# A spectral convolution's mode mix with x stationary and weights streaming, in a four-layer kernel on one core

## The chip, the core and the metric

The kernel runs on one core of a Trainium2 chip. The core has a matrix engine (TensorE, PE; its loads of the stationary operand are listed apart as PEld), a vector engine (DVE), a scalar engine (ACT), GpSimd (POOL), a queue engine (SP) that issues DMA transfers, and 16 DMA engines that all queues share. SP, ACT and POOL each have a queue of transfers of their own. The metric is the device time of one execution in microseconds (us). All data are float32; a float32 matmul of the program appears in the trace as two load and matmul pairs.

## The reference, cut to what matters

The input x is 8 x 32 x 256 x 256. Four layers follow one another, each adding to x a function of its group-normalised value. The change lies in the first and touches the start of the second:

```python
def _L0_conv_ref(x, w1r, w1i, w2r, w2i, bias):      # x: group-normalised
    w1 = w1r + 1j * w1i                              # 32 x 32 x 32 x 32: in, out, ky, kx
    w2 = w2r + 1j * w2i
    x_ft = jnp.fft.rfft2(x)
    out_lo = jnp.einsum('bixy,ioxy->boxy', x_ft[:, :, :M1H, :M2H], w1)
    out_hi = jnp.einsum('bixy,ioxy->boxy', x_ft[:, :, -M1H:, :M2H], w2)
    ...
    out = jnp.fft.irfft2(out_ft, s=(h, w))
    return out + bias
...
x = x + _L0_conv_ref(_gn(x), ...)                    # layer 0
x = x + _L1_conv_ref(_gn(x), L1_conv_kernel, 1, 2)   # layer 1: one 5 x 5 kernel for every channel
```

So for each of 64 x 32 modes there is a small complex product: 8 batches by 32 input channels, times 32 x 32 weights of that mode. Layers 2 (a recurrence over columns) and 3 (running maxima in four directions and a 1 x 1 convolution) are not touched.

## The kernel before, in words

**Forward (forward_and_mix, L75).** Work goes in 64 units: 8 batches of 8 units of 4 channels. A unit's x is 1 MB; `load(u)` (L113) brings it on SP into a ring of AHEAD = 7 buffers. `over_columns(u)` (L118) makes 16 matmuls (L131), one sum of squares on ACT (L140) and one on DVE (L141), and a transpose of the result on DVE (L144). `over_rows` (L148, matmuls at L158) transforms the second axis for the batch before, in four slices, so a batch's units 0 to 3 carry a slice each; its stationary operand is the table `fh` (1 MB, loaded at L107). `turn` (L166) transposes, `statistics` (L179) finds mean and scale, and `normalise` (L198) scales by DVE (L201), writes the modes with a sign to `xf[:, 0]` by ACT (L202), and the swap of real and imaginary parts to `xf[:, 1]` by four DMAs on POOL (L206). Lines L210 to L245 write the order of all this out by hand: every engine executes its instructions in that order.

**Constants (load_consts, L39).** SP issues eleven loads of constants first (L44), then `fh`, and then x.

**Mix (L247 to L290).** kx goes in 8 groups q of KC = 4. The weights of a q are 2 MB: q=0 has a pool of its own and is loaded in the last forward batch (L216); the next five buffers take space that the forward has to release first, and are loaded in a row when it ends (L253); two more follow. For each ky, pair of kx and half s (low or high ky), one matmul (L269) has the weights as its stationary operand (64 rows, 2 kx x 32 outputs) and x's modes as the moving one (32 columns: real and imaginary, batch, 2 kx). ACT (L286) and DVE (L284) copy the results out of PSUM into `sm`, two buffers per half, and SP and ACT store them to the DRAM tensor `smd`, laid out `[B, 2, KM, C, 2, KM]`: pieces of 256 B.

**Inverse and convolution (inverse_and_conv, L297).** `load_spectrum(b)` (L346) reads the modes of a batch back: 64 rows at once (L351), and the same with real and imaginary parts exchanged, in pieces of 128 B, in two more DMAs (L353). `turn` negates a half (L358), `means` (L364) and `spectrum` (L367 to L381) work on the zero mode. The tile's name in the profile is spec. `over_rows` (L403) then uses slices of spec as the stationary operand of the matmuls tp (L410), 512 instructions in all, and `over_columns` (L419) finishes the inverse transform (up, L427) and adds x, read a second time as xb (L388, issued on POOL, six DMAs of 786 KB for a unit). `conv` (L478) is layer 1. The order is again written out by hand, L613 to L689: spectra 0 and 1, the first unit's xb, then the first tp.

The DMA of the constant `bias` (L322) stands ahead of the spectrum loads in SP's queue, and its tile reuses space of the mix.

Of the kernel before, what the change touches and what calls it, by code (L numbers as in the profile page):

```python
# [38 lines left out]
def load_consts(tc, pool, d):  # L39
    nc = tc.nc  # L40
    k = Consts()
    for name in ("sign", "sel", "msel", "fw", "gw", "eh", "ident", "ident32", "pair", "valid", "conv"):
        t = pool.tile(list(d[name].shape), F32, name=f"c_{name}")
        nc.sync.dma_start(out=t, in_=d[name])  # L44
        setattr(k, name, t)
# [29 lines left out]
def forward_and_mix(tc, k, d, smd, xmean):  # L75
# [12 lines left out]
    with ExitStack() as ctx:  # L88
        one = ctx.enter_context(tc.tile_pool(name="m1", bufs=1))
        wp = ctx.enter_context(tc.tile_pool(name="mw", bufs=1))  # L90


        xf = one.tile([P, 2, B, KM, KM], F32, name="xf")
        wts = {}

        def load_weights(q, wp):
            wts[q] = wp.tile([P, KM, KC, C], F32, name=f"wt_{q}", tag="wt")
            nc.sync.dma_start(out=wts[q].rearrange("p y j o -> p (y j o)"), in_=d["wm"][q])

        with ExitStack() as inner:  # L100
            fwd = inner.enter_context(tc.tile_pool(name="a1c", bufs=1))
            xp = inner.enter_context(tc.tile_pool(name="a1x", bufs=AHEAD))
# [4 lines left out]
            nc.sync.dma_start(out=fh, in_=d["fh"])  # L107
# [90 lines left out]
            def normalise(b):  # L198
                xb, rs = turned.pop(b)
                xb = xb.rearrange("p y x -> p (y x)")  # L200
                nc.vector.tensor_scalar_mul(xb, xb, rs)  # L201
                nc.scalar.activation(xf[:, 0, b].rearrange("p y x -> p (y x)"), xb, AF.Copy, scale=k.sign)  # L202
                for s in range(2):
                    for ri in range(2):
                        r, r2 = 64 * s + 32 * ri, 64 * s + 32 * (1 - ri)
                        nc.gpsimd.dma_start(  # L206
                            out=xf[r : r + 32, 1, b].rearrange("p y x -> p (y x)"), in_=xb[r2 : r2 + 32]
                        )

            with tc.manual_schedule(engines=None):  # L210
                for u in range(AHEAD - 1):
                    load(u)
                for u, (b, n) in enumerate(units):
                    if u + AHEAD - 1 < len(units):
                        load(u + AHEAD - 1)
                    if b == B - 1 and n == 2:  # L216
                        load_weights(0, wp)
# [10 lines left out]
                    if b == B - 1 and n == NK - 2:  # L228
                        for i in range(SLICES):
                            over_rows(b, i, 0, NK // 2)  # L230
                for i in range(SLICES):
# [15 lines left out]
        wp2 = ctx.enter_context(tc.tile_pool(name="mw2", bufs=5))  # L247
        sp = ctx.enter_context(tc.tile_pool(name="ms", bufs=2))
        ps = ctx.enter_context(tc.tile_pool(name="mp", bufs=4, space=PSUM))
        NQ = KM // KC  # L250
        KY = KM // 2
        with tc.manual_schedule(engines=None):
            for q in range(1, 6):  # L253
                load_weights(q, wp2)
            for q in range(NQ):
                if 2 <= q < 4:
                    load_weights(q + 4, wp2)
                wt = wts.pop(q)
                mps = [
                    [ps.tile([P, 2 * B, 2, KY], F32, name=f"mp_{q}_{s}_{h}", tag=f"mp{s}") for h in range(2)]  # L260
                    for s in range(2)
                ]


                for ky in range(KM):
                    for j in range(0, KC, 2):
                        for s in range(2):
                            r = slice(64 * s, 64 * s + 64)
                            nc.tensor.matmul(  # L269
                                mps[s][ky // KY][32 * j : 32 * j + 64, :, :, ky % KY],  # L270
                                lhsT=wt[r, ky, j : j + 2, :].rearrange("p j o -> p (j o)"),
                                rhs=xf[r, :, :, ky, KC * q + j : KC * q + j + 2].rearrange("p r b x -> p (r b) x"),
                                start=True,
                                stop=True,
# [1041 lines left out]
```

## Time and profile before

| what | us |
|---|---|
| time of three runs, median (lowest to highest) | 3023.08 (3022.15 to 3023.44) |
| the profiled execution: its time | 3029.68 |
| the profiled execution: span from first to last instruction | 3027.8 |
| first x has landed, first matmul | 14.6 |
| last matmul of the forward's row transform ends | 208.1 |
| mix: first matmul; from here without a break | 216.37; 217.35 |
| mix: last matmul ends, first xb issued | 293.1, 293.66 |
| first load of a spectrum issued | 310.38 |
| first tp matmul | 321.44 |

Over the whole span PE is busy 92%, DVE 85%, ACT 62%, POOL 29%; the granted PE clock is 0.96 of full speed in the mean. Times in views are us from the start of the span, unless a number is marked ns. In the windows view a row is one stretch, with the busy time and the number of instructions of each engine; PEclk is the clock granted to PE. A line of the waits view says which engine's instruction at which line sat waiting for what, in total, how often, and the longest. Two passes make a matmul, so 1024 matmuls of the mix are 2048 instructions. Matmuls overlap in the array, so an instruction's own duration is longer than the time from one to the next. Beside the views, the trace has a record of every DMA packet: its start, queue, size and the time that it took.

### The profile page before, as it was taken

The page shows a single profiled execution, that of the slowest core. Times are in us where ns is not written, and L with a number is a line of the kernel's source. Part 1 is how long each engine was busy: PE and PEld are TensorE (multiplying, and loading weights), DVE is VectorE, ACT ScalarE, POOL GpSimd, SP SyncE. Part 2 cuts the span into 40 slices and gives each one's busy share as a digit, 9 for nine tenths or more (in the row PEclk, how much of TensorE's full clock was granted, in tenths as well). Part 3 has the DMA queues.
Part 4 walks back from the last instruction along what each step waited for, and adds up shares of the span by engine and source line. Part 5 has one row for each costly group of instructions (what it writes and reads, how often), then busy time and mean ns, then how long its engine had stood idle before and what let it go on. Part 6 is the DMA issues. An engine that isn't in the chain of part 4 may idle for free.

```text
span 3027.8 us, 111688 instructions
## 1 busy us (share of the span) xinstructions
PE 2784.2 (92%) x47736; PEld 1643.4 (54%) x47736; DVE 2578.6 (85%) x5161; ACT 1864.6 (62%) x4471; POOL 886.4 (29%) x1270
## 2 busy tenths in 40 slices
PE   7986799999999899999999999999999588888887
PEld 4656344444444566666666666666666333333333
DVE  5753578788788699999999999999999999999997
ACT  3432477767777688888888888888888232222222
POOL 0110122112221555555555555555555300000000
PEclk9995899999999899999999999999999799999998
DMA  9977678777776576566766566556764598888885
GB/s 386 392 274 241 181 214 241 227 216 228 220 224 173 140 169 154 141 142 156 169 145 142 141 164 162 143 141 148 169 153 114 185 376 326 323 325 326 331 333 225
DMA packets 470049, 655.69 MB, mean 217 GB/s; under 512 B 328016, under 2 KB 332000, under 8 KB 443312
## 3 DMA queue, kind: packets, MB, share of 16 engines
q1 hardware_dynamic: 410112, 484.48, 55.0%
q0 software_dynamic: 16224, 82.28, 8.2%
q10 hardware_dynamic: 43216, 81.79, 7.6%
q8 instruction: 374, 6.13, 0.8%
q14 instruction: 123, 1.01, 0.1%
HBM read 371.63 MB, written 272.63 MB: 213 GB/s over the span
## 4 chain that ended last, share of the span: by engine, by line
PE 66%; DVE 19%; issue 4%; DMA 2%; ACT 1%; SPq 0%; POOL 0%; DVEq 0%; ACTq 0%; POOLq 0%
PE r L784 14%; PE z L784 13%; PE vp L498 12%; PE ni L784 7%; PE nh L784 7%; DVE rv L1070 4%; PE up L427 4%; DVE dq L1085 2%; DVE uq L1087 2%; DVE m L1096 2%; DVE m L1093 2%; DVE m L1090 2%; PE tp L410 2%; PE mp L269 2%; PE o L1102 1%
## 5 line engine op out<-in xcount | busy, mean ns | idle before, releaser
L792 PE MATMUL z<-hs,weights 64*64 64x256 f32 x4080 | 539.4, 382 | 0.0
L792 PE MATMUL r<-hs,weights 64*64 64x256 f32 x4080 | 525.5, 375 | 0.0
L876 POOL TENSOR_TENSOR xw<-xw,hs 128x256 f32<-128x256 f32 x496 | 340.0, 686 | 632.8 <-DVE hs L875 629.7
L792 PE MATMUL ni<-hs,weights 64*64 64x256 f32 x4080 | 524.9, 375 | 0.0
L1128 ACT ACTIVATE ot<-o,bres 128x512 f32<-128x512 f32 x256 | 155.1, 688 | 493.4 <-PE o L1102 478.8
L498 PE MATMUL vp<-x,c_conv 64*64 64x384 f32 (+5 forms) x4608 | 424.2, 490 | 7.9 <-DVE x L531 7.9
L531 DVE SCALAR_TENSOR_TENSOR x<-vp,r,x 128x128 f32<-128x128 f32 (+2 forms) x640 | 350.4, 562 | 89.6 <-PE vp L498 77.5
L868 POOL TENSOR_TENSOR a<-zm,xn 128x256 f32<-128x256 f32 x510 | 373.0, 731 | 4.3 <-ACT zm L861 4.3
L866 ACT ACTIVATE n<-n,bih 128x256 f32<-128x256 f32 x510 | 259.2, 508 | 182.8 <-DVE n L865 182.8
L784 PE MATMUL r<-hs,weights 64*64 64x256 f32 x2040 | 319.1, 389 | 1.1
L498 PEld LDWEIGHTS vp<-x,c_conv 64*64 64x64 f32 x4608 | 222.2, 132 | 179.5 <-issue 101.5
L784 PE MATMUL z<-xn,weights 64*64 64x256 f32 x2040 | 305.3, 376 | 9.8 <-ACT xn L764 9.8
L1102 PE MATMUL o<-m,wsc 32*32 32x512 f32 x3072 | 226.2, 713 | 95.8 <-DVE m L1096 92.9
L784 PE MATMUL r<-xn,weights 64*64 64x256 f32 x2040 | 305.8, 376 | 0.0
L784 PE MATMUL nh<-xn,weights 64*64 64x256 f32 x2040 | 305.7, 376 | 0.0
L784 PE MATMUL z<-hs,weights 64*64 64x256 f32 x2040 | 305.4, 376 | 0.0
L784 PE MATMUL ni<-hs,weights 64*64 64x256 f32 x2040 | 305.2, 375 | 0.0
L764 ACT ACTIVATE xn<-xw,shift,turned 128x256 f32<-128x256 f32 x492 | 288.2, 586 | 0.0
L792 PEld LDWEIGHTS ni<-hs,weights 64*64 64x64 f32 x4080 | 284.4, 133 | 0.3
L860 DVE SCALAR_TENSOR_TENSOR n<-nh,bhh,rs 128x256 f32<-128x256 f32 x510 | 246.3, 483 | 43.1 <-ACT rs L859 28.2
L792 PEld LDWEIGHTS r<-hs,weights 64*64 64x64 f32 x4080 | 281.2, 131 | 0.2
L859 ACT ACTIVATE rs<-r,brz 128x256 f32<-128x256 f32 x510 | 241.7, 474 | 58.9 <-PE r L792 36.7
(171 smaller groups left out, 6243.4 us busy)
## 6 DMA issues: line engine op xcount, KB each, us to landing
xb<-in_xl_dram POOLq DMA_DIRECT2D x96, 768.0 KB, 7.2
xa<-in_xt_dram SPq DMA_DIRECT2D x64, 1024.0 KB
fwd<-fm SPq DMA_DIRECT2D x256, 256.0 KB
out_dram<-ot ACTq DMA_DIRECT2D x64, 1024.0 KB
xw<-x2d SPq DMA_DIRECT2D x248, 256.0 KB
fw<-fwd SPq DMA_DIRECT2D x31, 2048.0 KB
x3d<-xw SPq DMA_DIRECT2D x240, 256.0 KB
x<-x3d SPq DMA_DIRECT2D x30, 2048.0 KB
```

The source lines that it names most:

```text
L498: ins = nc.tensor.matmul(vps[bank][to, :, dst], lhsT=k.conv[r, P : P + 64] if kind == 2 else k.conv[r, o], rhs=pair_of(u, ch, g, lo, hi, s ...
L531: nc.vector.scalar_tensor_tensor(x, src[o], r1[rows, g : g + 1], x, ALU.mult, ALU.add, accum_out=s1[rows, 0, n, ch, g : g + 1])
L764: nc.scalar.activation(norms[bi][:, b, w], raws[bi][:, b, w], AF.Identity, bias=shift[:, b : b + 1], scale=sc[:, 1, b : b + 1])
L784: ins = nc.tensor.matmul(out[r], lhsT=weights[r, kind, gate, :], rhs=src[r], start=start, stop=stop)
L792: ins = nc.tensor.matmul(out[pairs[1 - i]], lhsT=weights[r, kind, gate, :], rhs=prev[r, :, q0 : q0 + Q], start=False, stop=stop,)
L859: rs = nc.scalar.activation(r, p["r"], AF.Sigmoid, bias=brz[:, 0:1])
L860: nc.vector.scalar_tensor_tensor(m, p["nh"], bhh[:, 2:3], r, ALU.add, ALU.mult)
L866: nc.scalar.activation(m, m, AF.Tanh, bias=bih[:, 2:3])
L868: product = nc.gpsimd.tensor_tensor(a, zm, cur, ALU.mult)
L876: nc.gpsimd.tensor_tensor(raw, raw, new, ALU.add)
L1102: nc.tensor.matmul(banks[bi][b2][i][32 * j : 32 * j + 32].rearrange("p (w q) -> p w q", q=Q), lhsT=wsc[q, b2, t, :], rhs=src[j][q, b2], st ...
L1128: nc.scalar.activation(ot[:, i], banks[bi][b2][i], AF.Identity, bias=bres[:, b2, i : i + 1])
```

## The change

- **Mix.** The stationary operand is now x's modes: for one ky and one q, 64 rows by 64 columns (real and imaginary, 8 batches, 4 kx), contiguous in a new layout of `xf`. The moving operand is the weights of the four kx, 128 columns. The result holds every x of the four kx against every weight of the four; only the blocks with equal kx are stored. A q is worked in two blocks c of 1 MB of weights, each in two groups of 4 ky per half.
- **Weights in x's ring.** Weights come in 16 halves of 1 MB through the same seven buffers and the same queue as x: seven halves behind the last x, each further one when a block of the mix has released a buffer.
- **Results.** A group's results are copied with one instruction for each s (128 x 512) into a stage tile, two buffers per s; `smd` is laid out `[2, KM, 2, 2, B, KM // 2, C]`, so that a stored row is 2 KB; eight DMAs of 64 KB for a q, four on SP and four on POOL. A spectrum is read in rows of 2 KB; the first on three queues. tp's stationary operand is then a slice with a step of 32 elements.
- **Order.** `fw` and six units of x are issued ahead of `fh`; three small constants follow between x's loads, the others and `bias` behind the weights at the forward's end. The first unit's xb is issued on SP within the mix (q = 5), from a pool of its own. The halves of `xf` with real and imaginary parts exchanged are made by copies on ACT (in the last batch on DVE, POOL and ACT) and not by DMAs. The first spectrum's half is negated on ACT.
- **Pools.** Those of the convolution wait for single tiles (`reuse_waits="tile"`).

```diff
-        nc.sync.dma_start(out=t, in_=d[name])
-        setattr(k, name, t)
+        setattr(k, name, pool.tile(list(d[name].shape), F32, name=f"c_{name}"))
+    k.bias = pool.tile([P, C], F32, name="bias0")
+    def load(*names):
+        for name in names:
+            nc.sync.dma_start(out=getattr(k, name), in_=d[name])
...
-        xf = one.tile([P, 2, B, KM, KM], F32, name="xf")
+        xf = one.tile([P, KM, KM // KC, 2, B, KC], F32, name="xf")
...
+        def load_weights(i):
+            if i < 2 * NQ:
+                q, h = divmod(i, 2)
+                wts[i] = xp.tile([P, 2, KY // 2, KC, C], F32, name=f"wt_{q}_{h}", tag="xa")
+                size = KY * KC * C
+                nc.sync.dma_start(
+                    out=wts[i].rearrange("p h y j o -> p (h y j o)"), in_=d["wm"][q, :, h * size : (h + 1) * size]
+                )
...
-                        nc.gpsimd.dma_start(
-                            out=xf[r : r + 32, 1, b].rearrange("p y x -> p (y x)"), in_=xb[r2 : r2 + 32]
-                        )
+                        out, src = xf[r : r + 32, :, :, 1, b], xb[r2 : r2 + 32]
+                        if b < B - 1 or s and ri:
+                            nc.scalar.copy(out, src)
+                        else:
+                            (nc.gpsimd if s else nc.vector).tensor_copy(out, src)
...
+                k.load("fw")
                 for u in range(AHEAD - 1):
                     load(u)
+                nc.sync.dma_start(out=fh, in_=d["fh"])
+                small = ["sign", "sel", "msel"]
                 for u, (b, n) in enumerate(units):
                     if u + AHEAD - 1 < len(units):
                         load(u + AHEAD - 1)
-                    if b == B - 1 and n == 2:
-                        load_weights(0, wp)
+                        if u > 1 and small:
+                            k.load(small.pop(0))
+                    else:
+                        load_weights(u + AHEAD - 1 - len(units))
...
+                load_weights(AHEAD - 1)
+                k.load("gw", "eh", "ident", "ident32", "pair", "valid", "conv")
+                nc.sync.dma_start(out=k.bias, in_=d["b0"].partition_broadcast(P))
...
             for q in range(NQ):
...
+                stage = [sp.tile([P, KC, KY, C], F32, name=f"sm_{q}_{s}", tag=f"sm{s}") for s in range(2)]
+                for c in range(2):
+                    wt = wts.pop(2 * q + c)
+                    for i in range(0, KY // 2, 4):
+                        mps = [ps.tile([P, 4, KC, C], F32, name=f"mp_{q}_{c}_{i}_{s}", tag=f"mp{s}") for s in range(2)]
+                        for y in range(4):
+                            for h in range(2):
+                                for s in range(2):
+                                    r, to = slice(64 * s, 64 * s + 64), slice(64 * h, 64 * h + 64)
+                                    ky = KY * h + KY // 2 * c + i + y
+                                    nc.tensor.matmul(
+                                        mps[s][to, y].rearrange("p j o -> p (j o)"),
+                                        lhsT=xf[r, ky, q].rearrange("p r b x -> p (r b x)"),
+                                        rhs=wt[r, h, i + y].rearrange("p j o -> p (j o)"),
+                                        start=True,
+                                        stop=True,
+                                    )
...
+                            dst, src = stage[s][:, :, ky : ky + 4], mps[s].rearrange("p y j o -> p j y o")
                             if s:
                                 nc.vector.tensor_copy(dst, src)
                             else:
                                 nc.scalar.copy(dst, src)
+                    load_weights(AHEAD + 2 * q + c)
+                if AHEAD + 2 * q in (2 * NQ, 2 * NQ + 1):
+                    for i in range(3):
+                        xb(0, 0, 0, i, nc.sync)
+                for s in range(2):
+                    for m in range(KC):
+                        (nc.sync, nc.gpsimd)[m % 2].dma_start(
+                            out=smd[s, KC * q + m].rearrange("h r b y o -> (h r b) (y o)"),
+                            in_=stage[s][m::KC, m].rearrange("p y o -> p (y o)"),
+                        )
...
+def conv_x(nc, d, pool):
...
+    def load(u, b, h, i, queue):
+        lo, hi = 3 * i, 3 * i + 3
+        for ch in range(2):
+            t = pool.tile([P, hi - lo, CH, Q], F32, name=f"xb_{u}_{ch}_{i}", tag=f"xb{ch}{i}")
+            queue.dma_start(
+                out=t.rearrange("p t c q -> p (t c q)"), in_=d["xl"][b, 2 * h + ch, :, lo * CH * Q : hi * CH * Q]
+            )
...
         def load_spectrum(b):
...
+            t = spp.tile([P, 2, 2, KM // 2, C], F32, name=f"spec_{b}", tag="spec")
+            queues = (nc.sync, nc.scalar, nc.gpsimd) if b == 0 else 3 * (nc.scalar if b > 1 else nc.sync,)
+            modes = smd[:, :, :, :, b].rearrange("s x h r y o -> (s x) h r (y o)")
+            flat = t.rearrange("p h r y o -> p h r (y o)")
+            queues[0].dma_start(out=flat[0:64].rearrange("p h r n -> p (h r) n"), in_=modes.rearrange("p h r n -> p (h r) n"))
             for ro in range(2):
-                queue.dma_start(out=t[64:128, :, ro], in_=modes[:, :, 1 - ro])
+                queues[ro + 1].dma_start(out=flat[64:128, :, ro], in_=modes[:, :, 1 - ro])
...
-                        lhsT=specs[b][:, 2 * CH * h + CH * ch + c + j].rearrange("p r y -> p (r y)"),
+                        lhsT=specs[b].rearrange("p h r y c -> p (h r y) c")[:, :, 2 * CH * h + CH * ch + c + j],
...
-            for i in range(3):
-                load(0, i)
-            turn(0, nc.vector)
+            half = specs[0][64:128, :, 1]
+            nc.scalar.activation(half, half, AF.Copy, scale=-1.0)
```

The host's layouts of the weights and of the table `gw` follow the new order; the amount of data is the same.

## The prediction

> **What bounds the kernel now.** I cut the span into stages with the windows view (us; busy time and count of PE, PEld, DVE, ACT, POOL; granted clock; DMA share; GB/s):
>
> ```profile
> 0.00:14.63 14.63, 0.00 (x0) 0.00 (x0) 0.91 (x7) 1.28 (x1) 2.02 (x7) 1.00 0.81 280
> 14.63:216.37 201.74, 186.97 (x3234) 119.46 (x3235) 136.72 (x266) 82.12 (x136) 26.89 (x40) 0.99 0.92 358
> 216.37:293.10 76.73, 57.53 (x2048) 55.71 (x2048) 25.22 (x60) 21.88 (x61) 0.00 (x0) 0.52 0.72 243
> 293.10:321.44 28.34, 0.61 (x2) 0.50 (x2) 3.35 (x11) 1.39 (x4) 3.37 (x8) 0.50 0.91 242
> 321.44:950.00 628.56, 618.60 (x7154) 291.99 (x7154) 507.77 (x1585) 445.37 (x1362) 120.10 (x153) 1.00 0.75 219
> ```
>
> These are: waiting for the first x; the forward transform; the mix; a gap in which smd is stored and read back; the convolution. Only these are touched. The convolution is 98% PE: nothing but a slower PE, or a later start, matters there. So the start of its first matmul (tp, 321.44) is the number to predict; everything later moves with it.
>
> The forward by batches of 8 units, then the waits (engine, line, who ended them: total, times, longest):
>
> ```profile
> 14.70:36.80 22.10, 18.44 (x289) 10.62 (x289) 15.78 (x26) 10.28 (x18) 0.00 (x0) 1.00 1.01 426
> 60.30:83.80 23.50, 23.03 (x396) 14.53 (x392) 17.02 (x34) 10.23 (x17) 3.56 (x5) 1.00 1.01 389
> ```
> ```profile
> PE y L364 <- DMA spec<-smd: 25.5, 1, 25.5
> PE yp L131 <- DMA xa<-in_xt_dram: 18.4, 7, 14.7
> ACT sm L286 <- DMA smd<-sm: 9.5, 1, 9.5
> SPq L322 <- DMA smd<-sm: 14.4, 1, 14.4
> ```
>
> The first batch goes at the pace of x (1 MB in 2.44 us by the arrivals, 426 GB/s); from the second on PE is the bound (23.03 of 23.50). PE waits 14.7 us for the first x and 25.5 for the spectrum. The third line is a store of q=0, still under way when its buffer is wanted at q=2: it was issued at 225.2, while five weight loads of 2 MB from 217.5 on stood in the DMA engines.
>
> **Part by part**, against the profiled execution (3029.68 us, span 3027.8; the shown median is 3023.08, 6.6 less; I carry the difference over).
>
> 1. *First x ahead.* Now SP issues 11 constants and fh before x, from 0.75 to 6.40, and x lands at 14.63. After: fw, then x. SP issues x at about 1.2; in the packet records data follow some 1.4 us after an issue; 1 MB takes 2.44, the 384 KB of recurrence weights beside it 0.9, and before, a landing showed 1.0 after its last packet: 7.0. That is 7.6 earlier, but fh now stands between x number 6 and 7, in the batch that goes at x's pace: 2.44 back. **-5.2.** (Bounds: 0, if the second batch were to wait for fh, to -7.6.)
>
> 2. *xf by copies.* Four POOL DMAs a batch become four ACT copies of 32x1024. The nearest row is the sign copy (L202, 1.15 us): 4.6 a batch. ACT is busy 10.24 of 23.50 and sits in front of the ring, waiting for x; the ring of 7 gives back what one late release costs, since x needs 8 x 2.44 = 19.5 of 23.5. So 0. Runs of 4 elements are new: at twice the price, 9.2, it still fits in the 13.3 that are free; from 3.3 us a copy on it would cost. In the last batch two copies go to DVE, one to POOL, one to ACT. POOL's row (L358, 1024 elements) is 2.78: from the end of DVE's scaling (212.68) dense mixing can start at about 215.8 instead of 217.35. **-1.6.**
>
> 3. *The mix itself.* 2048 PE instructions of 64x32 become 1024 of 64x128 (8 x 2 x 2 x 4 x 2 x 2 matmuls, two passes each). Now the first 254 took 6.31 us, 24.8 ns each, later ones 28.4 (128 in 3.64): a floor of an instruction and not of its columns. The recurrence issues 1824 instructions of 64x256 in its windows row 1500 to 1600, 54.8 ns each at clock 1.00; half the columns: 27.4. So 1024 x 27.4 = 28.1 us, and 56 at clock 0.50. Which clock?
>
> ```profile
> 212.70:222.90 10.20, 6.67 (x220) 6.33 (x221) 2.15 (x6) 2.60 (x5) 1.99 (x4) 0.51 0.65 202
> 222.90:226.30 3.40, 1.45 (x81) 1.26 (x73) 1.68 (x4) 1.45 (x4) 0.00 (x0) 0.97 1.01 424
> 226.30:293.00 66.70, 50.11 (x1766) 48.65 (x1765) 21.86 (x52) 18.91 (x52) 0.00 (x0) 0.50 0.70 235
> ```
>
> The clock came once, after 5.5 us of the densest stretch, and stayed at 0.50 through 66.7 us in which PE was busy 75%. With four times the columns per instruction the array has work all the time at 0.50, so I take cold for 5.5 us and warm after: 16 blocks, two or three of 3.4 us, then 1.85. [...]
>
> 4. *Its DMA is the new bound.* The ring holds 7 of the 16 half weights when mixing starts: their loads follow the releases of units 57 to 63. Left after that: 9 x 1.05 MB weights, 4.72 MB of conv's first xb (six of 786 KB, now queued on SP at q=5), 4.19 MB of stores: 18.4 MB at 0.42 MB/us, 43.7 us. The first release comes at 3.4, data 1.5 later: all moved at about 48.5, while PE alone could be done at 33. Stores of 2 KB rows: such packets (x2d) took 84 ns in the convolution, 24 GB/s an engine, near the 26.5 of 8 KB packets. In the recurrence they took 152, which would add 8 us. I take 84, the same direction and kind.
>
> 5. *The tail.* SP's half of the stores of q=5 is queued behind xb in the same ring. Stage tiles are double, so the evacuation of q=7 waits for them, as L286 did for 9.5 us above: to about 49. Then 4 copies of 128x512 (0.68, row of L436: 2.7), four issues on POOL (0.55 each, 2.2), a landing (2.2 at best for xf): 56.5 after the start of mixing. The spectrum: rows of 2 KB on three queues; 1 MB, plus half of the next spectrum, 3.6 at 0.42, and 2.2 to land: 62. Now 8.1 from issue to landing. The turn leaves DVE (0.69) for ACT beside it; of the 2.9 to the first tp 2.0 are left: **64.** Now it is 321.44 - 217.35 = 104.1. **-40.1.** Bounds: 57 if the q=5 stores don't hold up q=7 (48.5 + 1 + 7.5); 72 with 152 ns packets.
>
> 6. *tp's stationary operand strided* (128 B between columns; now contiguous). 512 instructions, all in the PE-bound convolution. No row shows a strided weight load. Nearest, a moving operand: means (L364) reads 32 columns 256 B apart:
>
> ```profile
> L364 PE MATMUL s<-spec,c_dc x12: 282/293/304, 444.9 to 866.3; 128*128 128x32 f32 x12
> L410 PEld LDWEIGHTS tp<-c_eh,spec x512: 132/137/232, 321.4 to 930.4; 128*64 128x64 f32 x171
> ```
>
> Contiguous, 4 columns took 257 (L460) and 16 took 265 (L574): at the 0.83 ns a column that the 54.8 ns imply (four tiles at once, 256 columns), 32 should take 280. So 13 ns for 32, some 26 for 64 weights: at most 13 us over 512 loads, were nothing hidden. Far end: the old mix read its moving operand in pairs 4 KB apart within 4 x 28.4 ns per 32 columns, 3.5 ns each; at that price a load costs 200 ns more, 100 us. I take 0: tp runs at 126 ns an instruction (8 in 1.01 us) and loads 137 beside it.
> [...]
>
> 7. The rest: bias moved (it stood behind the 14.4 us wait of SP, which the stores caused): nothing of its own. Spectra of 2 KB instead of 128 B rows on ACT's queue save issue time (L353, 2.6 us each, 12 times), off the path: PE's waits in the convolution come to 7.6 us, on DVE. 0, at best -7. The gw, eh, conv constants (0.8 MB) go to the end of the forward, behind the ring: eight issues of 0.45 on SP, over some 9 us before mixing; what queues behind them is the eighth weight load, which has to wait for mixing anyway, and tp needs them 60 us later. Within the mix SP alternates weight loads that wait for the ring with stores; a store is held up only by loads that its own blocks release.
>
> Sum: -5.2 - 1.6 - 40.1 = **-46.9**: 2982.8 profiled, **2976** beside the shown median.
>
> **Rivals.**
> - *Shorter tail* (q=5's stores don't matter, or PE is late enough to hide xb): -54, 2969, and with the 7 of part 1 and 7 in full 2960. For it: packets of two rings mix. Against: L286's wait.
> - *DMA or clock worse*: 2 KB packets at 152 ns (+8), or clock 0.50 throughout (mix 56, the last stores 4 to 5 later), or part of the strided load (+13): 2981 to 2997. For it: the 66.7 us at 0.50.
> - *The strided weight load decides; slower than before.* Place: 512 loads of tp. It takes back 46.9 from 92 ns a load on, if fully exposed. At 200 ns: 3023 + 55 = 3078. For it: 98% PE; against: L364.
> - *It doesn't do what it says*: the transfers of this stage keep their old pace of 243 GB/s, as small stores and weights go on hindering each other. Then 18.4 MB take 75.7 instead of 43.7, tp starts at 96 instead of 64, and -14.9 is left: 3008. Against: 424 GB/s while the five weight loads ran alone, and stores of 256 B, the hindrance, are gone.
>
> **Numbers.** Forecast with its own bounds (2964 to 2985) 0.60; shorter tail below 2964 0.10; worse DMA, clock or partly strided, and the old pace (2985 to 3016) 0.22; little change 0.02; strided load slower 0.06. Faster 0.92, same 0.02, slower 0.06; 0.2%, 6 us, is what a measurement can tell. Eight in ten: 2958 to 2998; about 0.05 lies below, 0.07 between its end and no change, 0.08 at no change and above.
>
> **What would show it.** First yp near 7 (else part 1); forward batches still 23.5; mix of 1024 instructions in about 41 us with PE waiting for wt or for stage tiles; DMA above 400 GB/s until the end of xb; first tp near 275 and convolution of 628 us after it. A tp rate above 126 ns an instruction is the strided load; a mix dense at clock 0.50 is the clock; a long wait of y for spec with DMA quiet is the tail mis-sized.

## The result and the profile after

The changed kernel takes 2980.37 us (median of 4 runs, 2979.01 to 2983.02); the kernel before takes 3023.26 beside it (3022.15 to 3024.62). The ratio is 0.9859, with a 95% interval of 0.9842 to 0.9876: 42.9 us less. The profiled execution took 2983.02 (span 2981.2) where that of before took 3029.68 (3027.8): 46.6 less. The forecast was 2976, and 46.9 less for the profiled pair.

The windows view cut into the same stages (us; busy time and count of PE, PEld, DVE, ACT, POOL; granted clock; DMA share; GB/s):

```profile
0.00:6.28 6.28, 0.00 (x1) 0.04 (x2) 0.60 (x5) 1.40 (x2) 2.02 (x7) 1.00 0.67 230
6.28:211.96 205.68, 188.51 (x3234) 119.54 (x3235) 138.97 (x270) 112.93 (x165) 12.46 (x9) 0.98 0.93 369
211.96:257.20 45.24, 35.96 (x1024) 32.83 (x1024) 17.94 (x28) 14.95 (x28) 15.01 (x28) 0.91 0.90 330
257.20:282.58 25.38, 0.61 (x3) 0.50 (x3) 3.49 (x10) 3.11 (x5) 2.90 (x7) 0.57 0.65 204
282.58:911.14 628.56, 626.04 (x7238) 307.15 (x7242) 513.43 (x1604) 448.63 (x1374) 121.50 (x154) 1.00 0.72 219
```

The first matmul comes at 6.28 instead of 14.63, the mix (third row) lasts 45.2 instead of 76.7 at a clock of 0.91 instead of 0.52, and the first tp comes at 282.58 instead of 321.44. The last row is as long as the fifth of before, but PE is busy 626.04 in it instead of 618.60. The lines of the waits view that answer to those shown of before, and two of SP's queue in the mix:

```profile
PE y L404 <- DMA spec<-smd: 23.1, 1, 23.1
PE yp L142 <- DMA xa<-in_xt_dram: 11.7, 5, 6.3
ACT sm L298 <- DMA smd<-sm: 28.8, 5, 13.4
DVE sm L296 <- DMA smd<-sm: 33.0, 6, 12.4
SPq L307 <- DMA wt<-in_wm_dram: 10.8, 7, 2.3
SPq L307 <- DMA xb<-in_xl_dram: 10.3, 6, 3.5
```

PE's wait for the first x went from 14.7 to 6.3. The copies out of PSUM wait much more for stage tiles than before. By this view the last two lines are stores (L307) that wait to be issued until earlier transfers of weights and of xb have landed, although they share no data with them. PE itself waits in the mix for the copies that free its PSUM tiles, and for no load of weights:

```profile
PE mp L285 <- ACT sm L298: 5.7, 5, 1.6
PE mp L285 <- DVE sm L296: 2.7, 3, 1.7
```

By stages, from the starts and ends of the same instructions in both traces:

| stage | change, us | forecast |
|---|---|---|
| start to the end of the row transform (208.12 to 203.60) | -4.5 | -5.2 |
| from there to the first dense matmul of the mix | -0.9 | -1.6 |
| from there to the first tp (104.1 to 70.6) | -33.5 | -40.1 |
| first tp to last tp (608.5 to 601.1) | -7.4 | 0 |
| the rest | -0.4 | 0 |

So the sum is right to within 0.3 us, and two terms in it are wrong by about 7 us each, with opposite signs: that it comes so near is luck. The experiments ask why the terms are off.

### The profile page after: what moved, and what is told of

It is laid out like the page before. It is cut to its first block, busy times and chain, and to the rows that moved or that the text cites. A ratio compares the mean times of both kernels' runs of the same rounds, so it can differ in the third digit from the quotient of the medians.

```text
span 2981.2 us, 109664 instructions
## 1 busy us (share of the span) xinstructions
PE 2763.3 (93%) x46712; PEld 1633.7 (55%) x46712; DVE 2572.6 (86%) x5130; ACT 1888.7 (63%) x4469; POOL 885.0 (30%) x1266
## 4 chain that ended last, share of the span: by engine, by line
PE 71%; DVE 20%; DMA 3%; issue 2%; ACT 1%; SPq 1%; POOL 0%; ACTq 0%; DVEq 0%; POOLq 0%
PE r L815 14%; PE z L815 13%; PE vp L530 13%; PE ni L815 7%; PE nh L815 6%; PE up L459 5%; DVE rv L1101 4%; PE yp L142 3%; DVE dq L1116 3%; DVE uq L1118 2%; PE tp L442 2%; DVE m L1127 2%; DVE m L1124 2%; DVE m L1121 2%; PE sp L169 2%
## 5 line engine op out<-in xcount | busy, mean ns | idle before, releaser
L891 DVE SCALAR_TENSOR_TENSOR n<-nh,bhh,rs 128x256 f32<-128x256 f32 x510 | 246.1, 483 | 42.9 <-ACT rs L890 28.9
```

Of the source, the lines that this page charges most:

```text
L891: nc.vector.scalar_tensor_tensor(m, p["nh"], bhh[:, 2:3], r, ALU.add, ALU.mult)
```

## Experiments

Ratios are to the kernel before, beside which each kernel was timed. "Mix to tp" is the time between the starts of the first matmul of the mix and of the first tp. Where the mix is left as it is, mix to tp came out between 66.0 and 70.6 in four profiled executions (the changed kernel, e2, e6, e7): a difference below 5 us in it says little. The medians of before differ by up to 6 us between the groups of runs, and the changed kernel was timed in the first group alone. So between it and e2 to e12 the ratios are the safer comparison: by them e4 gains 4 us on it, e8 9 us and e9 16 us, and e7 loses 8. The intervals of e9, e10 and e11 lie clear of the changed kernel's, those of e8 and e12 just meet it, and those of e2 to e7 overlap with it.

| kernel | median, us (lowest to highest) | ratio (95%) | mix to tp | first to last tp |
|---|---|---|---|---|
| before | 3020.47 to 3026.14 (medians of five groups) | 1 | 105.1 | 608.5 |
| after | 2980.37 (2979.01 to 2983.02) | 0.9859 (0.9842 to 0.9876) | 70.6 | 601.1 |
| e1, before with whole rows | 3018.12 (3015.69 to 3020.81) | 0.9986 (0.9976 to 0.9996) | 105.7 | 597.8 |
| e2, contiguous tp | 2978.59 (2974.17 to 2979.64) | 0.9852 (0.9834 to 0.9869) | 66.0 | 598.3 |
| e3, xb behind the stores | 2981.15 (2979.05 to 2981.53) | 0.9862 (0.9845 to 0.9879) | 69.2 | 600.7 |
| e4, xb ahead of the mix | 2974.84 (2973.53 to 2979.75) | 0.9845 (0.9827 to 0.9863) | 61.3 | 601.1 |
| e5, e4 with stores on POOL | 2976.09 (2974.54 to 2977.87) | 0.9845 (0.983 to 0.9859) | 61.7 | 600.9 |
| e6, ACT's copies twice | 2981.40 (2977.48 to 2985.24) | 0.9862 (0.9844 to 0.988) | 67.5 | 600.2 |
| e7, constants first | 2988.77 (2988.19 to 2990.49) | 0.9886 (0.9869 to 0.9902) | 70.0 | 601.3 |
| e8, xb behind the spectra | 2970.33 (2969.84 to 2974.12) | 0.9828 (0.9813 to 0.9843) | 55.6 | 600.5 |
| e9, e8 with more weights ahead | 2967.93 (2964.39 to 2970.52) | 0.9806 (0.9788 to 0.9825) | 54.7 | 600.8 |
| e10, e8 with spectrum 1 later | 2972.15 (2968.05 to 2974.54) | 0.9822 (0.9804 to 0.9839) | 56.2 | 600.1 |
| e11, e8 with four stage tiles | 2970.10 (2967.23 to 2973.18) | 0.9817 (0.98 to 0.9835) | 57.3 | 601.2 |
| e12, three stage tiles and weights | 2972.18 (2972.00 to 2974.57) | 0.9826 (0.981 to 0.9842) | 57.7 | 600.5 |

### e1: where the convolution's 7.4 us come from

In the trace of before, the waits view of the convolution has these two lines, and no DVE wait like the first one after the change; there the second has shrunk to the line in the second fence:

```profile
DVE x L436 <- DMA x2d<-x: 13.7, 3, 5.1
SPq L556 <- DMA spec<-smd: 28.6, 6, 8.5
```
```profile
SPq L588 <- DMA spec<-smd: 0.6, 1, 0.6
```

In the kernel before, SP's stores of results (x2d) stood behind spectrum loads that had been issued on ACT's queue in pieces of 128 B; DVE then found its x tile not yet stored, three times, and PE waited for DVE. The starts of tp show it: 64 of them take 82.9 us of the convolution's rhythm, but 87.1, 86.1 and 86.3 in the three steps with a stall. The experiment takes the kernel before and reads the spectra from the third on in whole rows of 8 KB. It leaves out the exchange of the real and imaginary parts in them.

```diff
-            for ro in range(2):
-                queue.dma_start(out=t[64:128, :, ro], in_=modes[:, :, 1 - ro])
+            if b > 1:
+                queue.dma_start(out=t[64:128], in_=modes)
+            else:
+                for ro in range(2):
+                    queue.dma_start(out=t[64:128, :, ro], in_=modes[:, :, 1 - ro])
```

> The kernel before, but the spectra of batches 2 to 7 come in two DMAs of whole 8 KB rows: real and imaginary parts are not exchanged in the second (this leaves out the exchange). Theory A: after the change the convolution ran 7.4 us shorter from the first tp to the last, because before it the pieces of 128 B kept the spectrum loads under way for long, SP's stores of x2d waited for them (28.6 us, 6 times), x1 tiles came free late, and DVE (13.7 us, 3 times, on x2d stores) and then PE stood still. Then those DVE waits go, first to last tp falls from 609.0 to about 599 us, and the kernel is 10 us (0.3%) faster than before, near 3013. Rival: the three stalls are chance of one profiled run or come from something else; then they are still there, or the time stays within 2 us of before.

Measured: both waits are gone, the steps are 82.93 to 82.99, and first to last tp falls by 10.7 us. So the cause of the stalls in this trace is shown. The timed gain is only 2.4 us by the medians, though (4.2 by the ratio). The kernel before ranges over 14 us in its runs beside this one (3017.6 to 3031.65), the edited one over 5. That fits stalls that come in some executions and not in others, of which the profiled execution of before, 6.6 above its median, was one that had them; no second trace of before is there to show it.

### e2: the strided stationary operand

The stationary operand of tp is taken contiguous again, 64 elements in a row. It leaves out the choice of the elements that the transform needs.

```diff
-    lhsT=specs[b].rearrange("p h r y c -> p (h r y) c")[:, :, 2 * CH * h + CH * ch + c + j],
+    lhsT=specs[b].rearrange("p h r y c -> p (h r y c)")[:, 64 * (2 * CH * h + CH * ch + c + j) :
+                                                           64 * (2 * CH * h + CH * ch + c + j) + 64],
```

> The changed kernel, but tp's stationary operand is 64 elements next to each other instead of 64 with a step of 32 (it leaves out the right choice of elements). In the changed kernel a load takes 189 ns instead of 137. Theory A: nearly all of that is hidden beside the matmuls; what shows is the step between two units of one batch, 83.24 us for every eight tp calls against 82.92 before, 5 ns a load, 2.6 us over 512 loads. So loads go back to 137 ns, the eight-call step to 82.92, the time falls by 2 to 3 us. Rival B: the 52 ns show in full, and it gains 20 us or more. Rival C: nothing shows, the 0.32 us have another cause; step stays at 83.24.

The load's line in the view of the tile tp (ns: min, median, max), first of the changed kernel, then of this one:

```profile
L442 PEld LDWEIGHTS tp<-c_eh,spec x512: 185/189/231, 282.6 to 884.2; 128*64 128x64 f32 x171
```
```profile
L442 PEld LDWEIGHTS tp<-c_eh,spec x512: 132/137/232, 278.0 to 876.8; 128*64 128x64 f32 x171
```

A load takes 52 ns more with a step of 128 B. Most of it is hidden beside other matmuls: a step of 64 tp takes 83.24 instead of 82.93, and first to last tp 601.1 instead of 598.3, some 5 ns for each of the 512 loads and 2.8 us in all. The median moves by 1.8.

### e3: xb behind the stores

```diff
-                if AHEAD + 2 * q in (2 * NQ, 2 * NQ + 1):
-                    for i in range(3):
-                        xb(0, 0, 0, i, nc.sync)
                 for s in range(2):
                     for m in range(KC):
                         (nc.sync, nc.gpsimd)[m % 2].dma_start(...)
+                if AHEAD + 2 * q in (2 * NQ, 2 * NQ + 1):
+                    for i in range(3):
+                        xb(0, 0, 0, i, nc.sync)
```

> The changed kernel, but the six loads of xb are issued behind SP's stores of q=5 instead of ahead of them. Theory A: the end of the mix is set by the double stage tile: q=7's copies wait for the stores of q=5 (12.4 and 13.4 us), which stand behind xb. Then those copies come right after q=7's matmuls, about 10 us earlier, the last stores some 5 us earlier (those of q=6 and q=7 on SP are still behind xb), and tp starts 4 to 6 us earlier: about 2975. Rival B: only the bytes count (18.4 MB must have moved before the last store); then the waits move but tp starts within 1 us of 70.6 after the start of mixing, and the time stays at 2980.

The longest wait for a stage tile falls from 12.4 to 4.8, as wanted, and the copies of q = 7 now follow the matmuls directly. It gains nothing: the last stores are issued behind xb instead. The waits view in the mix, and a piece of the chain:

```profile
DVE sm L296 <- DMA smd<-sm: 19.0, 5, 4.8
...
SPq L304 <- DMA xb<-in_xl_dram: 10.2, 5, 3.4
```
```profile
255.45 14.52 DMA xb<-in_xl_dram
269.99 1.77 DMA smd<-sm
```

So the stage tiles alone are not the cause; what stands ahead of the last stores is the suspect, and e4 and e8 move it.

### e4 and e5: xb ahead of the mix

e4 issues xb on SP before the first block of the mix; e5 in addition puts all stores of the mix on POOL.

```diff
+            for i in range(3):
+                xb(0, 0, 0, i, nc.sync)
             for q in range(NQ):
...
-                        (nc.sync, nc.gpsimd)[m % 2].dma_start(
+                        nc.gpsimd.dma_start(                      # e5 only
```

> The changed kernel, but xb is loaded ahead of the mix, in front of the eighth half of the weights. The DMA engines stood half idle in the first 10.5 us of the mix (179 GB/s, room for 2.5 MB). Theory A (stage tiles held by xb): nothing stands in front of the last stores any more, q=7's copies follow its matmuls, tp starts 10 to 14 us earlier: about 2968. Rival B (bytes alone): only the idle time is won, 6 us: 2974. Rival C: the weights behind xb come 11 us later than they could, PE waits for the eighth half, and what is won at the end is lost there: 2980 or more.

> As the run with xb first (it started tp 61.3 us after the start of mixing, and its matmuls took 47.2 us though PE was busy 36), and all stores of the mix are issued on POOL. Theory A: the matmuls are stretched because stage tiles wait for stores (DVE 21.9 us), and the stores are late because SP's issues stand behind its own earlier transfers (SP waited 14.5 us for weights before issuing stores, seven times) and in its ring. On POOL nothing stands ahead: PE is done by about 40 us, tp starts at 54 to 58, the time falls by another 3 to 7 us to about 2970. Rival B: the bytes decide; stores on POOL only shift the waits to weights, tp starts at 61 again. Rival C: eight issues of 0.55 on POOL behind each other cost 2.2 us at the end: 63.

Windows of e4:

```profile
213.00:223.00 10.00, 10.00 (x275) 9.96 (x278) 4.95 (x8) 4.25 (x8) 2.19 (x4) 0.74 1.02 421
223.00:248.00 25.00, 16.23 (x431) 14.74 (x426) 8.03 (x13) 6.59 (x13) 8.13 (x16) 0.88 1.01 391
```

The first 10 us of the mix, in which the changed kernel moves 179 GB/s because no buffer is free for weights, now carry xb at 421. Mix to tp falls by 9.4 and the median by 5.5 (4 us by the ratios). In e5 DVE's waits for stage tiles stay at 20.3 us and nothing is gained over e4, so SP's order isn't what holds back the remaining stores.

### e6: is ACT's copying of xf free?

```diff
-                            nc.scalar.copy(out, src)
+                            for _ in range(2 if b < B - 1 else 1):
+                                nc.scalar.copy(out, src)
```

> The changed kernel, with every ACT copy into xf of batches 0 to 6 issued twice: 4.2 us more a batch on ACT. Theory A: ACT's copies are hidden beside PE in the forward (ACT is busy some 15 of 23.4 us); step between batches stays at 23.4, end of the forward at 203.6, time 2980. Rival B: ACT has become a second bound through the ring of x (SP waits 41 us for ACT's squares now, 5.9 before): then each batch takes 1 us or more longer, 7 us or more in all.

The forward ends 0.9 us later, a difference that arises in its first two batches (25.1 and 23.9 us for 24.8 and 23.3); from the third on a batch takes 23.4 us in both. The median is 1.0 higher within ranges of 4 and 8 us. So the copies are hidden.

### e7: the constants ahead of x again

```diff
-                k.load("fw")
+                k.load("sign", "sel", "msel", "fw", "gw", "eh", "ident", "ident32", "pair", "valid", "conv")
+                nc.sync.dma_start(out=fh, in_=d["fh"])
...
-                nc.sync.dma_start(out=fh, in_=d["fh"])
-                small = ["sign", "sel", "msel"]
+                small = []
...
-                k.load("gw", "eh", "ident", "ident32", "pair", "valid", "conv")
```

> The changed kernel with all eleven constants and fh issued ahead of x again, as before. Theory A: the new order is worth what the first statistics show, 54.9 to 50.4: 4.5 us, so first yp near 15, tp 4.5 us later, time about 2985. Rival B: worth the whole 8.3 us by which the first x comes earlier: 2988. Rival C: nothing, because the weights' ring takes it up: 2980.

The row transform ends 5.3 us later and the first tp comes 4.7 later: the size that the forecast gave to this part. The median is 8.4 higher, which is the time that rival B gave, but not for B's reason: of the trace's 7.5 us the other 2.8 lie behind the first tp, and what puts them there stays open.

### e8: xb where it was before, behind the spectra

```diff
-                if AHEAD + 2 * q in (2 * NQ, 2 * NQ + 1):
-                    for i in range(3):
-                        xb(0, 0, 0, i, nc.sync)
...
             load_spectrum(0)
             load_spectrum(1)
+            for i in range(3):
+                load(0, i)
```

> The changed kernel with the first unit's xb where it was before, on POOL behind the loads of the spectra. Theory A: the 4.7 MB stood ahead of the last stores: without them tp starts 10 to 14 us earlier (57 to 60 after the start of mixing), but the first additions of x wait for xb, which comes 11 us after the spectra were asked for: from first to last tp it takes 5 to 10 us longer than 601, and the time ends near 2977. Rival B: xb was hidden where it was: tp starts at 70 as now, and the convolution still waits for xb: 2990.

Mix to tp falls by 15.0, to 55.6, and the median by 10.0. Windows of e8 from the eleventh us of its mix on:

```profile
222.30:242.30 20.00, 16.18 (x456) 14.24 (x452) 7.86 (x13) 6.42 (x13) 7.43 (x14) 0.91 1.01 406
242.30:258.70 16.40, 9.52 (x311) 8.55 (x301) 7.54 (x12) 6.45 (x12) 7.51 (x15) 0.99 0.60 229
```

4.72 MB at 0.42 MB/us (e4 moves xb at 421 GB/s) are 11.2 us, and that much traffic is out of the way of the last stores. I had expected the convolution to pay 5 to 10 us for the late xb. It doesn't: first to last tp is 600.5, and DVE waits for xb 0.5 us, since its first addition comes 7.7 us after the first tp. So this piece of the change is a loss of about 10 us, hidden inside a gain.

### e9 and e10: what is left of the tail

e9 gives weights 7 to 11 five buffers of their own, asked for when the mix begins; xb's pool is taken after the mix, to make room. e10 asks for the second spectrum on POOL behind xb, so that the first has the DMA engines to itself.

```diff
+        MORE = 5
...
+                pool, tag = (more, "wt") if AHEAD <= i < AHEAD + MORE else (xp, "xa")
...
+            for i in range(AHEAD, AHEAD + MORE):
+                load_weights(i)
             for q in range(NQ):
...
-                    load_weights(AHEAD + 2 * q + c)
+                    load_weights(AHEAD + MORE + 2 * q + c)
```
```diff
             load_spectrum(0)
-            load_spectrum(1)
             for i in range(3):
                 load(0, i)
+            load_spectrum(1)                                      # e10
```

> As the run with xb late (2970.3; tp 55.6 us after the start of mixing, PE done with the mix at 42.1), and halves 7 to 11 of the weights get five buffers of their own, asked for when the mix starts instead of when blocks release the ring. Theory A: the mix is bound by its transfers, which idle at its start (179 GB/s in the first 10 us) since a load has to wait for a release: 2.5 MB more can move there, 6 us; PE done at 36 to 38, tp at 50 to 52, time near 2966. Rival B: the stage tiles (17 us of waits for stores) set the pace of the mix, as every store shares the engines with weights: PE done at 42 again, nothing won.

> As the run with xb late, and the second spectrum is asked for on POOL behind xb instead of on SP beside the first. The first spectrum took 6.3 us from issue to landing. Theory A: its 512 reads of 2 KB are bound by their own 145 to 156 ns a packet (stores: 84), 4.8 us on 16 engines, and not by company: it lands at most 1 us earlier, time as before within 2 us. Rival B: the second spectrum shares the engines half and half: without it 2 to 3 us earlier, time near 2968.

e9's windows:

```profile
213.25:223.25 10.00, 10.00 (x281) 10.00 (x281) 5.28 (x8) 4.58 (x8) 2.18 (x4) 0.76 1.01 426
223.25:242.00 18.75, 12.02 (x329) 11.33 (x325) 6.16 (x11) 5.28 (x11) 5.53 (x11) 0.82 0.79 303
242.00:252.00 10.00, 10.00 (x366) 9.80 (x360) 6.76 (x11) 6.58 (x12) 5.72 (x12) 1.00 0.43 153
```

The weights come early, but the first stores come behind them: DVE waits 13.2 us for stage tiles, 9.6 of it at once, and the matmuls end 41.2 us after their start, as late as in e8 (42.1). PE stands still twice, 4.4 us for a stage tile and 2.9 us in a stop that no wait explains (e12 below shows its kind). e9 is the fastest kernel of the study by its median, 2.4 below e8, but the intervals of the two overlap. In e10 the first spectrum takes 6.9 us from its first issue to PE's first matmul on it, after 6.5 in e8: so the second spectrum was not what held it up. Its reads took longer than stores of 2 KB, which took 84 ns: SP's packets of 2 KB 86 ns in the median and 135 in the mean, ACT's 157, and POOL's of 4 KB 323. Together they are 4.7 us of 16 engines. The expectation had put 145 to 156 ns on all of them; more than half of SP's took 100 or less.

### e11 and e12: more stage tiles, and both

e11 is e8 with four stage tiles per half; e12 is e9 with three, and three extra weight buffers instead of five. In both, xb's pool is taken after the mix.

```diff
-        sp = ctx.enter_context(tc.tile_pool(name="ms", bufs=2, reuse_waits="tile"))
+        sp = ctx.enter_context(tc.tile_pool(name="ms", bufs=4, reuse_waits="tile"))   # e12: 3, and MORE = 3
```

> The run with xb behind the spectra, and four stage tiles per half instead of two (xb's pool is taken after the mix, so that there is room). There the copies waited 17.0 us (DVE) and 13.3 us (ACT) for stores to leave a stage tile, the last matmul of the mix ended 42.1 us after its first dense one, and tp started at 55.6. Theory A (the pair of stage tiles is what holds back the matmuls and, through the released weight buffers, the transfers): these waits go below 3 us, the matmuls end at about 37 (PE alone was forecast at 33), tp starts near 50.5, and the time is 5 us lower, about 2965. Theory B (the transfers' own pace: 9.4 MB of weights and 4.2 MB of stores from the first release on, at 393 to 419 GB/s, are 34 us after a first release at 3.4 and data 1.5 later): the waits go from the stage tiles to the weights, the matmuls end at 40 to 42, the last stores only 2 us later than now or at the same time, tp at 54 to 56, time 2968 to 2970.

> The run with xb behind the spectra, with three stage tiles per half instead of two and weights 7 to 9 in three buffers of their own, asked for when the mix begins. With five such buffers and two stage tiles the matmuls ended at 41.2 us and tp started at 54.7 us after the mix's first dense matmul, and the copies waited 13.2 and 12.7 us for stage tiles; the DMA engines were then idle by half in the second part of the mix. Theory A (stage tiles bind once the weights are early): the waits for stage tiles go below 5 us, the matmuls end near 36, tp starts near 49.5, time about 2962 to 2964. Theory B (the bytes bind; buffers only move the waits): matmuls end at 40 or later, tp at 53 to 55, time 2967 to 2969.

Both theories missed. The waits for stage tiles went (DVE has none left in e11 and e12; ACT 3.0 and 0.7 us), as A said, but the matmuls end 43.6 and 44.3 us after their start (e8: 42.1), and the first tp comes 1.7 and 2.1 later than in e8. Differences of that size say little, but the gain of 5 us that A forecast isn't there. Theory B named the weights; in e12 the DMA engines move 72 GB/s between 242.2 and 252.2 (third row below), so the bytes are not the reason either. Windows of e12, and its chain, which shows what is (start, us, what):

```profile
222.20:232.20 10.00, 6.26 (x151) 6.02 (x147) 3.19 (x6) 2.76 (x5) 2.14 (x4) 0.71 1.01 390
232.20:242.20 10.00, 6.35 (x190) 5.86 (x188) 3.79 (x6) 3.11 (x6) 4.29 (x8) 0.84 0.93 335
242.20:252.20 10.00, 10.00 (x292) 10.00 (x288) 6.17 (x9) 5.28 (x9) 2.82 (x6) 0.77 0.21 72
```
```profile
220.18 3.72 PE mp L288 x127
223.90 3.74 issue
227.64 6.39 PE mp L288 x127
234.03 0.11 issue
234.15 3.72 PE mp L288 x127
237.87 3.54 issue
241.40 16.25 PE mp L288 x488
```

PE works 127 instructions and then stands still for a time that the profile puts on no releaser. In e12 such stops come before matmuls 155, 282 and 536 (1.22, 4.01 and 3.81 us between starts), in e11 before 409, 663 and 790 (3.19, 1.88, 2.70). These numbers differ by multiples of 127, whatever the block or tile at that place. A matmul and its weight load are two instructions, so 127 are 254. In the packet records a queue that the profile names "instruction" moves one packet of 16 KB for each such stretch, and in e11 and e12 PE goes on 1.2 to 1.6 us after that packet's end, at every stop. While the data queues are full, the packet starts 3.1 to 5.1 us after PE has entered a stretch (at most other times 0.2 to 1.8), where at 27 ns an instruction PE needs 3.4 us for the whole of it. So PE's own program arrives late. That the transfers are what delays it is read from the times at which it is late: in e12 no stop comes once the DMA share has fallen to 0.21, and the packets there start 0.0 to 1.1 us after PE has entered a stretch. Without these stops (7.8 and 9.0 us) the matmuls would have ended at about 36 and 35, near what theory A gave; that last step is a subtraction, and no run took the stops away.

The kernel before has them as well, six in its mix, 17.0 us in all; at each PE goes on 1.4 to 1.5 us after the end of a packet of 16 KB. They can be read in its chain:

```profile
227.77 3.64 PE mp L269 x128
231.40 2.56 issue
233.96 3.63 PE mp L269 x96
237.60 2.33 issue
239.92 3.63 PE mp L269 x127
243.56 2.62 issue
```

The changed mix has half the instructions; its stops at these places come to 1.5 us in all. Its longer ones, up to 2.0 us, are at the limits of a q: PE waits for a copy to free a PSUM tile, and the copy for a stage tile. e9's stop of 2.9 us and one of 3.2 us in e4 are of the program's kind, both ahead of matmul 282.

## Why the prediction was right, and where it was not

The time and its range held, and so did the mechanism in the main: PE stopped being what bounds the mix, and its transfers took that place. Of the 33.5 us from the start of mixing to tp 30.5 lie in the mix (75.7 to 45.2) and 3.0 in the gap behind it (28.4 to 25.4). In the old mix PE's busy time (57.5) and the stops for its program (17.0) fill 74.5 of 76.7 us; in the new one PE is busy 36.0. No run changes the operands alone, so this share is read from the two traces. The windows of the changed kernel show the mix and the tail by their transfers, and the chain its end:

```profile
211.96:222.50 10.54, 10.28 (x283) 10.04 (x283) 5.53 (x8) 4.68 (x8) 2.32 (x5) 0.78 0.55 179
222.50:248.00 25.50, 17.64 (x488) 15.65 (x488) 7.97 (x13) 7.04 (x14) 8.42 (x16) 0.93 1.00 378
248.00:257.20 9.20, 8.05 (x256) 7.14 (x254) 4.45 (x8) 3.23 (x7) 4.28 (x8) 1.00 1.00 371
257.20:267.20 10.00, 0.01 (x1) 0.00 (x0) 0.00 (x0) 0.00 (x0) 0.00 (x0) 0.69 0.75 296
267.20:274.00 6.80, 0.00 (x0) 0.00 (x0) 2.48 (x4) 2.05 (x4) 2.14 (x4) 0.50 0.24 88
```
```profile
253.38 13.77 DMA smd<-sm
...
267.32 2.06 ACT sm L298 x4
...
271.18 2.18 DMA smd<-sm
...
274.38 7.08 DMA spec<-smd
281.45 0.02 issue
281.47 1.06 ACT spec L649
```

1. **First x ahead**: -4.5 for -5.2. x landed at 6.28, not 7.0; of the 8.4 us gained there the forward gave back 3.9, not 2.4. e7 gives 5.3 for the whole part.
2. **xf by copies**: -0.9 for -1.6. POOL's copy took 1.55 us, not 2.78, but PE's small matmul for the means, behind DVE's two copies (0.68 and 1.43) and its sum by group, has to run before the mix. ACT's copies are hidden (e6).
3. **The mix on PE**: right. Where nothing holds it up (e9, third row) 366 instructions take 10.00 us, 27.3 ns each, for 27.4; the clock is 0.50 in the first 4.6 us, for the 5.5 that I took from the old mix, then 1.00 for 5.9 (0.78 over the first row), and 0.93 and 1.00 after. What the granted clock goes by, no run shows: that it would come and stay was an estimate from the old mix's windows. What I had read into the old mix was incomplete, however: PE's idle quarter there, which I put on short columns, is in good part 17.0 us of waiting for its program.
4. **DMA as the bound**: the volume was right (the five rows come to 18.5 MB, for 18.4), the pace wrong. I took 0.42 MB/us; from 222.5 to 257.2 it was 0.371 to 0.378, and 0.296 behind that. At the forecast end, 48.5 us into the mix, 2.6 MB were still to come. Why a full set of engines moves 378 and not 420 stays open: packets of 8 KB took 345 ns in the mean from 222.5 to 248, and 310 in e9 where it moved 426 GB/s. That stretch and e4's at 421 have no 2 KB stores beside them, where these are 11% of the bytes; but e8's at 406 has 10%, so they aren't the whole reason. It is not weights that hold PE up: it waits for stage tiles, and so for stores.
5. **The tail**, with the mix ahead of it: -33.5 for -40.1; this is the term that was mis-sized. The trace shows the chain that was given: SP's store of q = 5 takes 13.77 us behind xb, the copies of q = 7 wait for its tile until 267.3, the last stores end 61.4 us after the start instead of 56.5, PE has the spectrum 6.9 after that instead of 5.5, and 2.3 instead of 2.0 remain to tp. (The forecast's own steps to the last store come to 56.1.) But the reason is another than I put it: e3 breaks this chain and gains nothing. Not the stage tile decides but the 4.72 MB ahead of the last stores in the same engines (e8, -15.0; e4, -9.4).
6. **The strided load**: 2.8 us for 0, inside the bounds of 0 to 13. With 52 ns it stays below the 92 from which it would have decided. The step of 128 B takes the load from 137 to 189 ns (e2), 0.8 ns for each of the 64 weights. (54.8 ns by four tiles over 256 columns are 0.86 ns a column, not 0.83; it moves the bound of 13 by less than 1.)
7. **The rest**: -7.4 in the profile, where I had written 0, at best -7. I had looked at whether PE waits for spectra, and not at who stands behind them: SP's stores, then DVE's tiles, then PE (e1, -10.7). Part 6's 2.8 stand against it in the same row.

By the profile, the errors of 5 and 7 cancel. In the timed runs they don't, because the stalls of 7 seem to have been a matter of the profiled execution (e1's timed gain is 2.4 to 4.2): I carried its distance of 6.6 to the median over to the changed kernel, whose own is 2.6. That is the 4 us between 2976 and 2980.

Of the rivals, the second came in part: the transfers were slower, by an amount that still lay inside the forecast's own bounds. The shorter tail (57 us) didn't come under the first rival's condition, that the stores of q = 5 don't hold up q = 7 (e3: 69.2); it was to be had by leaving xb where it was (55.6 in e8). Packets of two queues do mix, which spoke for that rival: from 222.5 to 248 the changed kernel's 2350 packets (1821 on SP's queue, 525 on POOL's) change from one queue to another 690 times.

## What to carry to other kernels

A transfer that is issued early is not free: ask which later transfers it goes ahead of in the same engines, and whether the one that ends a stage is among them; here 4.7 MB that nobody waited for yet cost 10 us. A profiled execution above the median (by 6.6 us here) may hold stalls that a typical run lacks, so a term read from it may belong to it alone. Where PE stops at a fixed count of instructions with no releaser (here at steps of 127 matmuls with their loads, 17.0 us in the old mix), count its instructions, and look for its program's packets behind the data.

## What the runs showed of the hardware that was not expected

- PE's program comes in packets of 16 KB, on a queue that the profile counts among those of the 16 DMA engines. Beside full queues (330 to 437 GB/s) they start 3.1 to 5.1 us after PE enters a stretch of 127 matmul pairs, and PE stood still 1.2 to 4.0 us at a time: 17.0 us in the old mix, 7.8 in e11, 9.0 in e12. e11 and e12 each moved 8 such packets between 212 and 260 us, beside their mix of 1024 matmuls.
- Packets of 2 KB took 84 ns as stores of the mix; as reads of the first spectrum those on ACT's queue took 153 to 157 in the median (the changed kernel, e8 and e10), while more than half of those on SP's took 100 or less (the changed kernel and e10).
- Spectrum loads in pieces of 128 B on ACT's queue held back the stores of another queue by up to 8.5 us; in rows of 2 KB, by 0.6.
